# A graph network layer on one core: the short group of edges moved from the end to the start, and one set of nodes instead of two after the last edges

## The chip, the cores and the metric

The kernel runs on one core of a Trainium2 chip. The metric is the device time in microseconds (us), taken as the median of several runs. One further execution is recorded by the hardware profiler; its rows are the "trace" and its summary "the page". The engines are TensorE (PE; PEld is its weight load), VectorE (DVE), ScalarE (ACT), GpSimd (POOL) and SyncE (SP). "Granted clock" is the share of its full clock that TensorE was given.

## The reference

There are 6250 nodes with 256 features, and 206250 edges sorted by their target node (100000 edges in both directions and one loop per node). Everything is float32.

```python
h = relu(layernorm(x))                                # the layer's input
polarity = clip(edge_attr[:, 0:1], 0, 1); raw = edge_attr[:, 1:]          # 64 features of an edge
e = relu(raw @ W_e1.T + b_e1) @ W_e2.T + b_e2
edge_emb = (e * (polarity + 0.01)) @ W_le.T + b_le
msg  = relu(h[src] + edge_emb)
aggr = segment_sum(msg, dst, num_segments=6250)
g = (h + aggr) @ W_g1.T + b_g1
out = x + relu(layernorm(g) * ln_g + ln_b) @ W_g2.T + b_g2
```

## The kernel before

**Tiles.** An edge tile is 128 edges. Four tiles make a block (`S = 4`), six blocks a group (`L = 6`, 3072 edges), and two blocks a pair, which is what one load of `raw` brings (256 KB, L237, on SP's queue). 206250 edges are 67 whole groups and 426 edges over, so there are 403 blocks, `NB = NF * L + 1`: group 67, the last, has one block, number 402, and the last pair (201) is half empty. A unit `u` is two tiles, half a block; there are 806 units.

**Work on an edge.** `first_layer(q)` (L239 to L261) multiplies a pair's raw features with `W_e1`, in four matmuls of 512 columns (L250); ACT writes three of the four results out (L259), DVE one (L256). `edge_part(u)` (L266) multiplies with the product of `W_e2` and `W_le` (L274), and DVE writes the message out with its bias (L279). In the first 22 units every third message is written by ACT without the bias (L277, `plain`), which DVE adds later (L607). `whole(u)` (L601) multiplies by the polarity and adds the gathered source row (DVE, L609, two steps), and ACT takes the relu (L614; for the last unit in two halves, L612). `add_up(b)` (L616) sums a block's edges by target: each of the four tiles is multiplied with a selector of 32 rows (L626), accumulated in PSUM over the group's blocks. The selectors are made by DVE, one step per block (L589), from each edge's row number within its group (`rel`, L488). When a group is complete, `keep(g)` (L633) copies its sums out (L638, or L640 for the last but one).

A matmul of float32 operands appears in the trace as two passes: a unit is 8 passes of L274, a pair's first layer 8 of L250, a tile of the sums 2 of L626.

**Order.** The order is written out by hand (`tc.manual_schedule()`), and each engine keeps it. At first, `LEAD = 22` units run beside the normalisation of the nodes, whose result goes to device memory (`hb_d`). From then on a loop runs over `u`: `forward(u)` (L306) does the unit and, when `u % 4 == TURN` (TURN = 1), a turn for pair `u // 4` (`turn_of`, L291): first layers two pairs ahead, the sums that are due, and loads four pairs ahead. In the middle of the run (`by_two`) every other turn does two pairs at once. After `forward`, the loop makes `whole` for units some distance behind (18 at first, 1 at the end), two per step until it has caught up, and one step of a queue of small jobs (`piece`, `due`). Among these are, right after the lead, `first_rows` (L479), `strips` (L768: `rel`, and the selectors of groups 0 and 1 are queued), and `row_numbers`. The selectors of group g + 2 are queued when group g's first block is summed. PSUM tiles come from a pool of seven (`psz`), and the two accumulators of the sums from another (`pd`).

**Source rows.** Rows `h[src]` are gathered from `hb_d` by POOL, 128 at a time (L560), in step with PE and at most 20 units ahead. The first four units' rows (`RAW`) are gathered from `x` itself and normalised separately (L460 to L466, L605).

**Nodes.** A set of nodes is 128 rows; the 49th has 106. A set is finished when the last group that can hold its edges is kept: `node_work(w)` (L674) makes selectors (L692), adds the groups' sums into the transposed node rows (`rows_of`, L720 to L728), and then runs three steps some units apart: `one` (`first`, L165: the matmul with `W_g1`, L170, bias, statistics, normalisation L180), `two` (`second`, L183: transposes L186, relu L189) and `three` (`third`, L193: matmul L196, the sum with x, L198, and the store, L201).

**The end.** Set 47 ends with group 66 and set 48 with group 67. Both are held back in `ending` and written out after the loop: the sums of set 47 (L726), the first part of those of set 48 (L710), `one` of set 47, the last block's sums, the second part of set 48, then `two`, `one` and `three` of the two in turn. For these two the bias `b_g1` is put into PSUM by a matmul of its own (L168) ahead of L170.

Of the kernel before, what the change touches and what calls it, by code (L numbers as in the profile page):

```python
# [33 lines left out]
NB = NF * L + 1  # L34
# [3 lines left out]
MARGIN = 768  # L38
DEG = E // N
# [16 lines left out]
def group_of(b):  # L56
    return b // L


def blocks_of(g):  # L60
    return range(g * L, min((g + 1) * L, NB))


def windows_of(g):

    lo = (GE * g - MARGIN) // DEG
    hi = (GE * (g + 1) + MARGIN) // DEG
    return [w for w in range(NW) if w * P <= hi and (w + 1) * P > lo]
# [29 lines left out]
def gnn_kernel(ctx: ExitStack, tc: tile.TileContext, x, src_c, dst_c, dst_r, pol_c, raw_t, w_e1t, w_e2,  # L98
# [50 lines left out]
    def finish_nodes(nd, ps, w, n):  # L149
# [15 lines left out]
        def first(aT, bias_by_pe=False):  # L165
            ph = ps()
            if bias_by_pe:
                nc.tensor.matmul(ph[:n, 0, :], ones[0:1, :n], bg1_b[0:1], start=True, stop=False)  # L168
            for c in range(2):
                nc.tensor.matmul(ph[:n, 0, :], aT[:, c, :n], wg1_s[:, c, :], start=c == 0 and not bias_by_pe, stop=c == 1)  # L170
            hs = nd.tile([P, D], F32, name="hs")
            if bias_by_pe:
# [7 lines left out]
            nc.vector.tensor_scalar(hs[:n], hb[:n], mv[:n, 0, 0:1], rs[:n], op0=ALU.subtract, op1=ALU.mult)  # L180
# [32 lines left out]
        return turn, first, second, third, load_x, offset  # L213
# [4 lines left out]
    with fast:  # L218
# [20 lines left out]
        def first_layer(q):  # L239

            bs = [b for b in (2 * q, 2 * q + 1) if b < NB]
# [5 lines left out]
            for c in range(2):  # L247
                for s, b in enumerate(bs):
# [4 lines left out]
            for c in range(2):  # L253
                for s, b in enumerate(bs):
# [7 lines left out]
        def plain(u):  # L262

            return u < LEAD and u % 3 == 1
# [41 lines left out]
        def forward(u):  # L306

            edge_part(u)
            if u % 4 == TURN:
# [19 lines left out]
        nc.scalar.dma_start(out=src_0, in_=src_c[:, :2 * RAW])  # L329
# [9 lines left out]
        nc.gpsimd.iota(mid, pattern=[[GE, NG]], base=GE // 2, channel_multiplier=0, allow_small_or_imprecise_dtypes=True)  # L339
# [4 lines left out]
        for u in range(RAW):  # L344
            hg[u] = hx_p.tile([P, 2, D], F32, name="hg")
            for i in range(2):
                nc.gpsimd.indirect_dma_start(
                    out=hg[u][:, i, :], out_offset=None, in_=x,
                    in_offset=bass.IndirectOffsetOnAxis(ap=src_0[:, 2 * u + i:2 * u + i + 1], axis=0))
        full = NF * L * S  # L350
# [4 lines left out]
        with tc.tile_pool(name="p1", bufs=4) as p1, tc.tile_pool(name="p1x", bufs=11) as p1x:  # L355
            parts = list(chunks())
            xts, mvs = {}, {}
            units = iter(range(LEAD))
# [97 lines left out]
            for n, u in enumerate(units):  # L456
                for m in range(n * RAW // 2, (n + 1) * RAW // 2):
                    row_stats(p1, P, 2, lambda i: hg[m][:, i, :], mv_0[:, 2 * m:2 * m + 2, :])
# [4 lines left out]
            for u in range(RAW):  # L463
                for i in range(2):
                    k = 2 * u + i
                    nc.scalar.activation(hg[u][:, i, :], hg[u][:, i, :], AF.Relu, bias=nm_0[:, k:k + 1],  # L466
# [12 lines left out]
        def first_rows():  # L479

            pb = ps().rearrange("p a b -> p (a b)")[:, :NG * S].rearrange("p (g j) -> p g j", j=S)
            nc.tensor.matmul(pb[:, :NF, :], ones[0:1, :],
                             dst_f[0:1, :full].rearrange("o (g r) -> o g r", r=L * S)[:, :, :S], start=True, stop=True)
            nc.tensor.matmul(pb[:, NF, :], ones[0:1, :], dst_f[0:1, full:], start=True, stop=True)
            nc.scalar.activation(base_b, pb, AF.Copy)

        def rows_of_edges():
            nc.vector.tensor_tensor(  # L488
                rel[:, :full].rearrange("p (g k j) -> p g k j", k=L, j=S),
                dst_f[:, :full].rearrange("p (g k j) -> p g k j", k=L, j=S),  # L490
                base_b[:, :NF, :].rearrange("p g (o j) -> p g o j", o=1).to_broadcast([P, NF, L, S]), ALU.subtract)
            nc.vector.tensor_tensor(rel[:, full:], dst_f[:, full:], base_b[:, NF, :], ALU.subtract)
# [21 lines left out]
        def by_group(i, op):  # L514
            def step():
                nc.vector.tensor_reduce(far[:, i, :NF], dst_f[:, :full].rearrange("p (g r) -> p g r", r=L * S),
                                        axis=AX.X, op=op)
                nc.vector.tensor_reduce(far[:, i, NF:], dst_f[:, full:], axis=AX.X, op=op)
            return step

        def by_row(i, op):
            def step():
                nc.vector.tensor_reduce(ends[:, i:i + 1], rel, axis=AX.X, op=op)
# [477 lines left out]
```

## Time and profile before

| | us |
|---|---|
| median of 3 runs | 2513.2 |
| lowest and highest run | 2512.73, 2515.78 |
| time of the profiled execution | 2537.35 |
| its span, first to last instruction | 2535.6 |
| TensorE busy | 2368.3 (93%) |
| VectorE busy | 1657.0 (65%) |
| POOL busy | 1634.3 (64%) |
| ScalarE busy | 983.4 (39%) |
| mean granted clock | 0.967 |

The page gives busy times over the whole span. The other views answer for a part: the timeline gives instructions in order of time, with the idle time before them and what ended it; the waits give these idle times grouped; the chain follows what ended last back in time; the windows give busy times and the granted clock by stretch. A busy TensorE is not one at its peak, and "issue" in a list of waits is time in which the engine waited for nothing that the profile shows.

### The profile page before, as it was taken

What the parts mean: (1) busy time and instruction counts of PE and PEld (TensorE: products, weight loads), DVE (VectorE), ACT (ScalarE), POOL (GpSimd) and SP (SyncE); (2) the same over time, 40 slices, a digit from 0 to 9 for tenths busy, and PEclk for the clock granted to TensorE, in tenths of its full rate; (3) what the DMA queues carried; (4) which work ended last, traced back from release to release, by engine and by line L of the source; (5) the groups of instructions that cost most, each with busy time, mean ns of one, the idle gap of its engine ahead of it and who ended that gap; (6) DMA issues with size and microseconds to landing.
All of it is one profiled execution on the core that took longest, in us unless ns stands there. A gap on an engine that the chain in (4) does not pass through costs nothing.

```text
span 2535.6 us, 35656 instructions
## 1 busy us (share of the span) xinstructions
PE 2368.3 (93%) x12382; PEld 1669.2 (66%) x12382; DVE 1657.0 (65%) x3975; ACT 983.4 (39%) x1710; POOL 1634.3 (64%) x1675
## 2 busy tenths in 40 slices
PE   9989999999999999999999999999999999999978
PEld 6666666676766666666766766666766666666646
DVE  7866566666767666665666666666766666666736
ACT  7433333333433433343333333333433333333313
POOL 7666666666666666666666666666666666666661
PEclk9999999999999999999999999999999999999979
DMA  9444344433443443434343444344334334433441
GB/s 308 132 119 121 105 126 119 125 119 106 120 134 115 126 119 102 132 112 127 120 129 112 127 117 120 107 123 121 117 115 128 118 113 118 126 115 109 121 117 41
DMA packets 156226, 309.23 MB, mean 122 GB/s; under 512 B 33327, under 2 KB 78088, under 8 KB 156040
## 3 DMA queue, kind: packets, MB, share of 16 engines
q0 software_dynamic: 77376, 211.39, 28.8%
q1 hardware_dynamic: 77364, 92.23, 11.6%
q10 hardware_dynamic: 1300, 3.28, 0.4%
q8 instruction: 98, 1.61, 0.3%
q14 instruction: 88, 0.72, 0.1%
HBM read 293.92 MB, written 12.85 MB: 121 GB/s over the span
## 4 chain that ended last, share of the span: by engine, by line
PE 86%; issue 6%; DVE 5%; another core or an unknown queue 1%; ACT 1%; DVEq 0%; ACTq 0%
PE pz L274 53%; PE pz L250 17%; PE pd L626 10%; PE pz L726 2%; PE pz L170 2%; PE pz L196 2%; DVE hg L609 2%; DVE msg L279 1%; ACT e L259 1%; PE pz L186 1%; DVE st L141 0%; DVE e L256 0%; DVE sel L589 0%; ACT xt L388 0%
## 5 line engine op out<-in xcount | busy, mean ns | idle before, releaser
L560 POOL DMA_INDIRECT hg<-hb_d,src_s x1604 | 1589.3, 991 | 842.5 <-issue 481.3
L274 PE MATMUL pz<-wc_s,e 128*128 128x256 f32 x6448 | 1484.4, 385 | 34.3 <-issue 26.7
L274 PEld LDWEIGHTS pz<-wc_s,e 128*128 128x128 f32 x6448 | 1220.1, 192 | 303.9 <-issue 95.2
L614 ACT ACTIVATE hg<-hg 128x512 f32<-128x512 f32 x805 | 507.1, 631 | 934.3 <-DVE hg L609 760.2
L279 DVE TENSOR_TENSOR msg<-pz,bc_s 128x512 f32<-128x512 f32 x799 | 547.1, 686 | 233.7 <-remote 86.8
L609 DVE SCALAR_TENSOR_TENSOR hg<-msg,pol_s,hg 128x256 f32<-128x256 f32 x1612 | 697.0, 480 | 0.4
L256 DVE TENSOR_SCALAR e<-pz,vecs 128x512 f32<-128x512 f32 x201 | 150.4, 748 | 568.7 <-PE pz L250 192.3
L250 PE MATMUL pz<-raw,we_s 64*128 64x512 f32 x1612 | 480.2, 661 | 24.3 <-issue 18.3
L259 ACT ACTIVATE e<-pz,vecs 128x512 f32<-128x512 f32 x605 | 376.3, 685 | 318.0 <-remote 112.9
L626 PE MATMUL pd<-hg,sel 128*32 128x256 f32 x3216 | 280.5, 389 | 82.8 <-issue 74.6
L250 PEld LDWEIGHTS pz<-raw,we_s 64*128 64x128 f32 x1612 | 170.5, 198 | 240.9 <-issue 176.4
L626 PEld LDWEIGHTS pd<-hg,sel 128*32 128x32 f32 x3216 | 116.0, 110 | 264.2 <-issue 215.0
L589 DVE SCALAR_TENSOR_TENSOR sel<-iota_w,zero_c,rel 128x128 f32<-128x128 f32 x403 | 138.6, 344 | 0.0
L638 ACT ACTIVATE ms<-pd 128x256 f32<-128x256 f32 x66 | 25.3, 384 | 257.9 <-PE pz L274 92.8
L726 PE MATMUL pz<-s,ms 128*128 128x128 f32 x548 | 74.6, 280 | 6.1 <-issue 5.6
L726 PEld LDWEIGHTS pz<-s,ms 128*128 128x128 f32 x548 | 71.1, 194 | 11.6 <-issue 7.7
L701 DVE SCALAR_TENSOR_TENSOR hT<-hT,zero_c,stb 128x128 f32<-128x128 f32 (+1 forms) x196 | 67.1, 343 | 2.3 <-issue 2.3
L170 PE MATMUL pz<-wg_s,hT 128*128 128x256 f32 (+1 forms) x196 | 51.6, 386 | 7.0 <-DVE hT L728 4.7
L196 PE MATMUL pz<-wg_s,nT 128*128 128x256 f32 (+1 forms) x196 | 51.2, 381 | 1.3 <-issue 0.6
L170 PEld LDWEIGHTS pz<-wg_s,hT 128*128 128x128 f32 (+1 forms) x196 | 36.1, 190 | 16.1 <-DVE hT L728 7.5
L196 PEld LDWEIGHTS pz<-wg_s,nT 128*128 128x128 f32 (+1 forms) x196 | 37.0, 190 | 7.7 <-issue 1.7
L392 POOL TENSOR_TENSOR hb<-xt,rows_b 128x256 f32<-128x256 f32 (+1 forms) x49 | 34.2, 729 | 12.0 <-issue 5.4
(98 smaller groups left out, 415.4 us busy)
## 6 DMA issues: line engine op xcount, KB each, us to landing
raw<-in_raw_t_dram SPq DMA_DIRECT2D x202, 256.0 KB
hg<-hb_d,src_s POOLq DMA_INDIRECT x1604
stb<-st_d SPq DMA_DIRECT2D x49, 128.0 KB
hb_d<-hb SPq DMA_DIRECT2D x12, 512.0 KB
xt<-in_x_dram SPq DMA_DIRECT2D x48, 128.0 KB
hT<-in_x_t_dram SPq DMA_DIRECT2D x48, 128.0 KB
out_dram<-ot SPq DMA_DIRECT2D x48, 128.0 KB
xt<-in_x_dram SPq DMA_DIRECT2D x11, 512.0 KB
```

The costliest lines, as they stand in the source:

```text
L196: nc.tensor.matmul(po[:n, 0, :], nT[:, c, :n], wg2_s[:, c, :], start=c == 0, stop=c == 1)
L250: z = nc.tensor.matmul(pe[s, c], we1_s[s * F:(s + 1) * F, c * P:(c + 1) * P], raw[q][s * F:(s + 1) * F, :], start=True, stop=True)
L256: nc.vector.tensor_scalar(e1[b][:, c, :], pe[s, c], be1_s[:, c:c + 1], 0.0, op0=ALU.add, op1=ALU.max)
L259: nc.scalar.activation(e1[b][:, c, :], pe[s, c], AF.Relu, bias=be1_s[:, c:c + 1])
L274: last_z = nc.tensor.matmul(pz[:, i, :], e1[b][:, c, k:k + P], wc_s[:, c, :], start=c == 0, stop=c == 1)
L279: nc.vector.tensor_add(msg[u], pz, bc_s)
L560: g = nc.gpsimd.indirect_dma_start(out=hg[u][:, i, :], out_offset=None, in_=hb_d, in_offset=bass.IndirectOffsetOnAxis(ap=src_s[:, 2 * u + ...
L589: nc.vector.scalar_tensor_tensor(sel[g][:, k * S:(k + 1) * S, :], iota_w.rearrange("p (o w) -> p o w", o=1).to_broadcast([P, S, W]), zero_ ...
L609: nc.vector.scalar_tensor_tensor(hg[u][:, i, :], m[:, i, :], pol_s[:, 2 * u + i:2 * u + i + 1], hg[u][:, i, :], op0=ALU.mult, op1=ALU.add)
L614: nc.scalar.activation(hg[u], hg[u], AF.Relu)
L626: z = nc.tensor.matmul(acc[g][j * W:(j + 1) * W, :], sel[g][:, k * S + j, :], m[:, j % 2, :], start=k == 0, stop=b == blocks_of(g)[-1])
L726: nc.tensor.matmul(pa[:, c, :n], ms[g][:, c * P:(c + 1) * P], box["sel2"][i][:, :n], start=i == 0, stop=i == len(gs) - 1)
```

## The change

The blocks are numbered anew. Block 0 is void: it has no edges and nothing is computed for it. Block 1, alone, is group 0 (the first 512 edges). Groups 1 to 67 have six blocks each, and the last of them holds the padding. Every group from the first on ends with a pair, the last pair (201) is full, and the first pair (0) has one real block. Units run from 2 to 807 (`U0 = 2`), still 806 of them; all that counted units from 0 now counts from `U0`. As pairs are still turned at `u % 4 == 1`, the first layer of pair q + 2 comes two units earlier, counted from the first unit, and the very first unit has a turn of its own. The first loop step after the lead is `u = 24`, so the first turn with two pairs comes at the 24th unit, where no sums are due yet; the first sums, of 20 tiles, come at the 32nd. Before, 8 tiles were summed at the 26th unit and 16 at the 34th.

At the end only set 48 is held back; the margin by which edges may lie before their expected place is cut from 768 to 512 for the last group, so that set 47 needs nothing of it and ends with group 66, which now closes six blocks before the last. Set 48's part from group 66 and its bias are put into PSUM before the last units' messages are whole. The last group's sums are copied half by ACT and half by DVE, and set 48's normalisation is done in two halves. The host lays out the edges accordingly. The core of the diff:

```diff
-NB = NF * L + 1
+NB = NF * L + 2
+SP = S * P
+LAST = 512
+U0 = 2
 def group_of(b):
-    return b // L
+    return (b + L - 2) // L
 def blocks_of(g):
-    return range(g * L, min((g + 1) * L, NB))
+    return range(max(1, 2 + (g - 1) * L), 2 + g * L)
 def windows_of(g):
-    lo = (GE * g - MARGIN) // DEG
-    hi = (GE * (g + 1) + MARGIN) // DEG
+    a, b = (SP + GE * (g - 1), SP + GE * g)
+    lo = (a - (LAST if g == NG - 1 else MARGIN)) // DEG
+    hi = (b + MARGIN) // DEG
...
+        def bias():
             ph = ps()
-            if bias_by_pe:
-                nc.tensor.matmul(ph[:n, 0, :], ones[0:1, :n], bg1_b[0:1], start=True, stop=False)
+            nc.tensor.matmul(ph[:n, 0, :], ones[0:1, :n], bg1_b[0:1], start=True, stop=False)
+            return ph
+        def first(aT, begun=None):
+            ph = ps() if begun is None else begun
...
-            nc.vector.tensor_scalar(hs[:n], hb[:n], mv[:n, 0, 0:1], rs[:n], op0=ALU.subtract, op1=ALU.mult)
+            for h in ([slice(0, P), slice(P, D)] if begun is not None else [slice(0, D)]):
+                nc.vector.tensor_scalar(hs[:n, h], hb[:n, h], mv[:n, 0, 0:1], rs[:n], op0=ALU.subtract, op1=ALU.mult)
...
-            bs = [b for b in (2 * q, 2 * q + 1) if b < NB]
+            bs = [b for b in (2 * q, 2 * q + 1) if 1 <= b < NB]
...
-            if u % 4 == TURN:
+            if u % 4 == TURN or u == U0:
                 turn_of(u // 4)
...
-            units = iter(range(LEAD))
+            units = iter(range(U0, U0 + LEAD))
...
+            nc.vector.tensor_scalar(far[:, 1, NG - 1:], far[:, 1, NG - 1:], float(MARGIN - LAST), None, op0=ALU.add)
...
-                    acc[g] = pd[:, g % 2, :] if g < NG - 1 else ps()[:, 0, :]
+                    acc[g] = pd[:, g % 2, :]
...
-                    if g != NG - 2:
-                        nc.scalar.activation(ms[g], acc.pop(g), AF.Copy)
+                    a = acc.pop(g)
+                    if g < NG - 1:
+                        nc.scalar.activation(ms[g], a, AF.Copy)
                     else:
-                        nc.vector.tensor_copy(ms[g], acc.pop(g))
+                        nc.scalar.activation(ms[g][:, :P], a[:, :P], AF.Copy)
+                        nc.vector.tensor_copy(ms[g][:, P:], a[:, P:])
...
+                def begin():
+                    sums_of(gs[:-1])
+                    box["ph"] = bias()
...
-                if gs[-1] < NG - 2:
-                    return lambda: at(now + 2, rows_of)
-                ending[gs[-1] - NG].append((sums_of, halves_out, rows_of, one, two, three, gs))
+                if gs[-1] < NG - 1:
+                    return lambda: at(now + 2 - (gs[-1] == NG - 2), rows_of)
+                ending.append((begin, sums_of, halves_out, one, two, three, gs))
...
-                lag = max(LEAST, LEAD - RAW - u // SHRINK) + (by_two(u // 4) and (u + 1) % 8 == TURN)
-                ready_for = min(u + 1 - lag, 2 * (u + 1 - LEAD))
+                lag = max(LEAST, LEAD - RAW - (u - U0) // SHRINK) + (by_two(u // 4) and (u + 1) % 8 == TURN)
+                ready_for = min(u + 1 - lag, U0 + 2 * (u + 1 - U0 - LEAD))
...
+            while steps:
+                steps.popleft()[1]()
+            for begin, sums_of, halves_out, one, two, three, gs in ending:
+                begin()
+            while made < NU:
+                whole(made)
+                made += 1
+            add_pairs(last=True)
+            for begin, sums_of, halves_out, one, two, three, gs in ending:
+                sums_of(gs[-1:])
+                halves_out()
+                one()
             while todo:
                 now = min(todo)
                 for fn in todo.pop(now):
                     fn()
-            while steps:
-                steps.popleft()[1]()
-            before, last = ending[-2], ending[-1]
-            for sums_of, halves_out, rows_of, one, two, three, gs in before:
-                rows_of()
-            for sums_of, halves_out, rows_of, one, two, three, gs in last:
-                sums_of(gs[:-1])
-            while made < NU:
-                whole(made)
-                made += 1
-            for sums_of, halves_out, rows_of, one, two, three, gs in before:
-                one()
-            add_pairs(last=True)
-            for sums_of, halves_out, rows_of, one, two, three, gs in last:
-                sums_of(gs[-1:])
-                halves_out()
-            for sums_of, halves_out, rows_of, one, two, three, gs in before:
-                two()
-            for sums_of, halves_out, rows_of, one, two, three, gs in last:
-                one()
-            for sums_of, halves_out, rows_of, one, two, three, gs in before:
-                three()
-            for sums_of, halves_out, rows_of, one, two, three, gs in last:
+            for begin, sums_of, halves_out, one, two, three, gs in ending:
                 two()
                 three()
```

More of the change, by code (lines that the diff above doesn't have):

```diff
@@ L211, in offset @@
             nc.vector.scalar_tensor_tensor(xt[:n, h], xt[:n, h], zero_c[:n], bg2_b[:n, h], op0=ALU.add, op1=ALU.add)
-        return turn, first, second, third, load_x, offset
+        return turn, bias, first, second, third, load_x, offset
     NU = 2 * NB
@@ L522, in step @@
             def step():
-                nc.vector.tensor_reduce(ends[:, i:i + 1], rel, axis=AX.X, op=op)
+                nc.vector.tensor_reduce(ends[:, i:i + 1], rel[:, S:], axis=AX.X, op=op)
             return step
@@ L679, in node_work @@
                 far_apart = (3, 5, 4) if gs[-1] < NG - 3 else (2, 3, 2)
-                turn, first, second, third, load_x, offset = finish_nodes(nd, ps, w, n)
+                turn, bias, first, second, third, load_x, offset = finish_nodes(nd, ps, w, n)
                 def spread():
@@ L928, in nodes @@
             nc.sync.dma_start(out=ac[:n], in_=acc_d[bass.ds(w * P, n), :])
-            turn, one, two, three, load_x, offset = v["finish_nodes"](sk, lambda: sp1.tile([P, 1, D], F32, name="ps_a"), w, n)
+            turn, _, one, two, three, load_x, offset = v["finish_nodes"](sk, lambda: sp1.tile([P, 1, D], F32, name="ps_a"), w, n)
             xt = load_x()
```

91 lines of the change are left out of this document (44 added, 47 removed).

## The prediction

> **What bounds the kernel now.** I read the page's first and fourth parts, then the list of waits of TensorE, then the stretches in which TensorE was not full: the start, the middle of the span and the end.
>
> ```profile
> span 2535.6 us, 35656 instructions
> ...
> PE 2368.3 (93%) x12382; PEld 1669.2 (66%) x12382; DVE 1657.0 (65%) x3975; ACT 983.4 (39%) x1710; POOL 1634.3 (64%) x1675
> ...
> PE 86%; issue 6%; DVE 5%; another core or an unknown queue 1%; ACT 1%; DVEq 0%; ACTq 0%
> ```
>
> TensorE (PE) is the bound, busy 93% of the span and 86% of the chain that ended last; DVE, ACT and POOL stay at 65% or less. The change leaves its work alone (the same 806 units of two edge tiles, the same first layers; two small matmuls of the last node sets and one bias fewer). So the time can move only where PE waits, or where something stands behind PE's last work. The waits:
>
> ```profile
> PE pd L626 <- issue: 74.6, 126, 1.7
> PE pz L274 <- issue: 26.7, 45, 1.7
> PE pz L250 <- issue: 18.3, 29, 1.7
> ```
>
> These 119.6 us are waits for nothing that the profile shows. One stretch is special (columns: stretch, its length, then busy time and count of PE, PEld, DVE, ACT and POOL, the granted clock, DMA share, GB/s):
>
> ```profile
> 2439.62:2470.59 30.97, 16.24 (x36) 9.34 (x36) 1.33 (x4) 2.04 (x4) 19.73 (x21) 0.52 0.32 93
> ```
>
> 36 matmuls at the 0.22 us step of the rows below need 7.9 us; 30.97 passed, 23.1 too many. The profiled execution took 2537.35 us, the median of the runs is 2513.2: 24.15 apart, about this one hole. I therefore take the hole as the profiled execution's own, make the sum as a difference against that execution (2537.35), and apply it to 2513.2.
>
> **Part 1: the start.** The rows of PE (start, duration, line, count of passes, idle time before and its releaser):
>
> ```profile
> 14.14 3.62 PE L274 MATMUL pz<-wc_s,e 128*128 128x256 f32 x16
> 18.69 1.99 PE L250 MATMUL pz<-raw,we_s 64*128 64x512 f32 x8 [0.93 <-DMA raw<-in_raw_t_dram]
> ...
> 64.96 1.99 PE L250 MATMUL pz<-raw,we_s 64*128 64x512 f32 x8
> ...
> 74.94 1.99 PE L250 MATMUL pz<-raw,we_s 64*128 64x512 f32 x8
> 80.74 0.64 PE L626 MATMUL pd<-hg,sel 128*32 128x256 f32 x8 [3.81 <-DVE sel L589]
> ...
> 84.69 2.45 PE L250 MATMUL pz<-raw,we_s 64*128 64x512 f32 x4 [0.50 <-DVE msg L279]
> ```
>
> A unit (8 passes) costs 3.62/2 = 1.8, a pair's first layer 1.9 to 2.0. At 18.69 PE waited 0.93 for the edge rows of pair 2. In the changed order PE has one block's first layer (0.95) and one unit (1.8) less to do before that load lands, because pair 0 holds one real block and pair 2 is asked for after one unit instead of two. The loads ahead of it on SP's queue are the same, so it lands when it did: PE waits 0.93 + 2.75 = 3.7 us. **Loss 2.75.** Nothing wins it back before 64.96, since PE was busy 45.44 of the 46.27 us from there on (columns as above):
>
> ```profile
> 18.69:64.96 46.27, 45.44 (x200) 33.56 (x200) 40.95 (x135) 37.28 (x79) 34.17 (x48) 1.00 0.92 311
> ```
> The later pairs' loads are issued one unit earlier relative to the work and stay covered.
>
> Then comes the one place where VectorE (DVE) bounds: 74.94 to 87.06. PE did 16 passes of L250 twice (2 x 1.92) and 16 of L626 (1.0) in 12.1 us: **7.3 us lost**, first for the row selectors of the first sums, then for PSUM tiles. DVE there (start, duration):
>
> ```profile
> 70.51 0.69 DVE L279 TENSOR_TENSOR msg<-pz,bc_s 128x512 f32<-128x512 f32 x1
> 71.11 0.68 DVE L605 TENSOR_TENSOR hg<-hg,rows_b 128x512 f32<-128x512 f32 x1
> 71.83 0.88 DVE L609 SCALAR_TENSOR_TENSOR hg<-msg,pol_s,hg 128x256 f32<-128x256 f32 x2
> 72.62 0.69 DVE L605 TENSOR_TENSOR hg<-hg,rows_b 128x512 f32<-128x512 f32 x1
> ...
> 80.25 0.35 DVE L589 SCALAR_TENSOR_TENSOR sel<-iota_w,zero_c,rel 128x128 f32<-128x128 f32 x1
> 80.51 0.69 DVE L279 TENSOR_TENSOR msg<-pz,bc_s 128x512 f32<-128x512 f32 x1
> ...
> 87.17 0.75 DVE L256 TENSOR_SCALAR e<-pz,vecs 128x512 f32<-128x512 f32 x1 [1.10 <-PE pz L250]
> ...
> 101.37 0.68 DVE L279 TENSOR_TENSOR msg<-pz,bc_s 128x512 f32<-128x512 f32 x1
> ```
>
> From start to start a message costs 0.60, a pair of L609 0.79, a selector 0.26. The message of the 23rd unit stands at 70.51, that of the 32nd at 101.37: 30.9 us for nine units, with 15 selectors and 13 pairs of L609 between them. In the changed order, counted from the instruction lists, there are 6 selectors (group 0 has one block, so 7 are due instead of 12, and group 2's come later) and 12 pairs: 9 x 0.26 + 0.79 = 3.1 less. The idle 1.10 goes, and a wait of about 0.5 comes, since the first layers of pairs 8 and 9 now follow each other with no sums between and eight tiles go into seven PSUM buffers. So 30.9 - 3.1 - 1.1 + 0.5 = 27.2. When DVE reaches the 23rd unit is between 0 (its own list sets it) and 2.75 later (PE's delay goes through); I take the middle, 1.4. The 32nd message then comes at 70.5 + 1.4 + 27.2 = 99.1, **2.3 earlier** than before. The first sums, now 20 tiles after the 32nd unit, find their selectors made. PE follows DVE there through its buffers, so I take -2.3 for PE. Bounds: +2.75 if PE is the bound and nothing is won back, 2.75 - 7.3 = -4.5 if the whole stall goes. The selectors put off fall where DVE has gaps.
>
> **The clock is the price.** Grid slices (columns as above):
>
> ```profile
> 78.95:82.36 3.41, 1.40 (x18) 0.56 (x20) 3.37 (x7) 0.18 (x1) 3.02 (x2) 0.99 0.26 77
> 82.36:85.77 3.41, 2.91 (x7) 1.12 (x8) 3.41 (x10) 2.60 (x5) 2.58 (x3) 0.50 0.32 84
> 85.77:89.19 3.42, 3.42 (x9) 1.77 (x6) 2.32 (x7) 2.31 (x5) 2.63 (x3) 0.51 0.39 113
> 584.09:587.50 3.41, 1.56 (x7) 1.41 (x8) 1.55 (x4) 2.31 (x4) 1.18 (x2) 1.00 0.19 59
> 587.50:590.92 3.42, 3.42 (x21) 3.12 (x21) 3.42 (x9) 1.89 (x3) 2.50 (x4) 1.00 0.27 77
> ```
>
> A slice in which PE was busy 1.40 of 3.41 is followed by two at half clock; one with 1.56 is not. So about 45% busy is the edge. The new wait of 3.7, or the waits for PSUM of about 2 near 75 and 95, will put some slice under it: one slice at half clock costs 3.41/2 = 1.7. Bounds 0 to three slices, 5.1. I take one. The start comes to -2.3 + 1.7 = **-0.6**.
>
> The Trainium skill, "TensorE: Matmul & The Clock Gate", Part 1, has PE throttled to half after at least one idle window of about 3.4 us. By that rule a wait of 3.7 would seldom hold a whole window, no slice would be lost, and the sum would end 1.7 lower. The slice at 78.95, with 41% busy, speaks against it.
>
> **Part 2: the end.** The chain of waits, and ScalarE's (ACT) rows:
>
> ```profile
> 2515.46 1.99 PE pd L626 x32
> ...
> 2518.01 1.16 PE pz L726 x8
> ...
> 2520.67 1.07 PE pz L170 x4
> ...
> 2523.07 0.69 PE pz L710 x4
> ...
> 2524.69 1.06 PE pz L170 x4
> ...
> 2526.98 0.56 DVE hs L180
> ```
>
> ```profile
> 2519.10 0.63 ACT L614 ACTIVATE hg<-hg 128x512 f32<-128x512 f32 x1 [2.87 <-DVE hg L609]
> 2520.36 0.75 ACT L612 ACTIVATE hg<-hg 128x256 f32<-128x256 f32 x2 [0.62 <-DVE hg L609]
> ...
> 2524.12 0.81 ACT L189 ACTIVATE nT<-pz,vecs 128x128 f32<-128x128 f32 x2 [1.10 <-PE pz L186]
> ```
>
> PE's last unit ends at T = 2515.46; the span ends 20.1 later. Two node sets stand in that tail now, one in the changed kernel.
>
> Moved ahead of T: 24 passes of sums (16 + 4 tiles stood behind T, 8 stay: 24 x 1.99/32 = 1.5), the set of nodes 47 with 8 passes of L726 (1.1) and L170 (1.07). T comes **3.7 later**; DVE and ACT keep up, because the chain of set 47 lies beside the last three units.
>
> Behind T in the new order: message (0.6), L609 of the last two units (0.8 each, the first frees ACT at T + 1.4), ACT's relu (0.63), then ACT's two steps for set 47, which stand ahead in its queue (0.81), the last relu in halves (0.75): T + 3.6. The last sums and the copy of the group, half on ACT and half on DVE (under 0.36), put the second matmul pair of the last set at T + 4.1, against 2523.07 = T + 7.6 before. From there 12.5 us remained. L170 then started 1.62 after it, because the bias stood between; with the bias ahead it starts after its first half is read, about 0.85: 0.8 less. The normalisation L180 (0.56) in halves lets transposes and nT start early: half a step, 0.5, an estimate (bounds 0 and 0.9). T + 4.1 + 12.5 - 1.3 = T + 15.3 against T + 20.1: 4.8 less. With T 3.7 later: **-1.1**, bounds -2.5 (the moved sums partly fill waits) and +0.5 (the halves bring nothing and ACT's queue holds the last relu).
>
> The rest is free: the void block's load lies on SP beside other work, one more scalar step in the check runs on DVE in a stretch with gaps; each index load has four columns more, against 1612.
>
> **Sum.** -0.6 - 1.1 = -1.7: 2535.65 on the scale of the profiled execution, 2511.5 on that of the runs.
>
> **Rivals.**
>
> *The instruction feed decides (slower).* q8 is PE's instruction queue:
>
> ```profile
> q8 instruction: 98, 1.61, 0.3%
> ```
>
> 98 blocks of 16.4 KB, 256 instructions each, and 119.6 us of "issue" waits, 1.2 us per block, most before L626, which uses up instructions fastest. The change shifts where blocks end against the sums by some 56 instructions (two units 32, one block's first layer 8, its sums 16, with weight loads). If six more blocks end in sums, each costs 1.2 and about half of them a clock slice (0.85): +12.3, 2523.8; from four on the result is over 0.2% slower. The same mechanism with six fewer gives 2499, so it is a draw around the forecast. For it: 200 such waits (126 + 45 + 29) stand against 98 blocks. Against: sums and blocks drift past each other several times in the run, which evens out. The Trainium skill, "Runtime: NRT & Kernel Launch", Instruction fetch mechanics, states the refill in blocks of 256 instructions and calls the crossing mostly hidden; by that the change could not move it. The 119.6 us are against hidden, but no row shows the fetch itself.
>
> *The start gains whole (faster).* No slice falls under 45% and the stall near 80 goes entirely: -4.5 at the start, -1.5 at the end, -6.0: 2507. For it: the grid's phase is open, and a wait cut in two by a slice's end may leave both above the edge. Against: 3.7 us is about the 3.81 of the L626 row that half clock followed.
>
> *Nothing comes of it.* PE keeps its total, the late start eats the tail: +2.75 + 1.7 - 1.1 and part of the stall won back: 2513 to 2516.5.
>
> **Chances.** Forecast with its own range (2508.2 to 2514.5) and the third rival, all within 0.2%, 0.43 together; start whole or fewer blocks in sums 0.37; feed on the slow side or two more clock slices 0.20. 0.2% (5 us) is about what a measurement of this kernel can tell from no change. The range reaches to both feed cases without their ends: 2502 to 2519.5.
>
> **What would show it.** After: an L250 near 18.7 with 3 to 4 us of idle before it, released by the raw load; no idle of 3.8 released by sel; the 32nd unit's message near 99; T to the end of the span 15.3; L168 ahead of the last L626. It fails if the issue sum moves by more than 8 us, or the clock in 15 to 30 us falls for two slices or more.

## The result and the profile after

The changed kernel took 2527.33 us (median of 9 runs, 2520.49 to 2533.47), the kernel before 2513.20 in the same series (2504.55 to 2517.68): ratio 1.0042, 95% interval 1.0026 to 1.0059. The medians lie 14.1 us apart; the ratio gives 10.6 us (6.5 to 14.8). Forecast were 2511.5 and a range up to 2519.5. The measurement was then repeated in further series, where the two kernels ran side by side each time:

| series | before, us | changed, us | ratio (95%) | PE waits for "issue" |
|---|---|---|---|---|
| first | 2513.20 | 2527.33 | 1.0042 (1.0026 to 1.0059) | yes |
| e9 | 2549.96 | 2550.85 | 1.0002 (0.9982 to 1.0021) | yes |
| e5 | 2180.94 | 2182.08 | 1.0006 (0.9997 to 1.0015) | none |
| e13 | 2180.43 | 2181.82 | 1.0008 (0.9999 to 1.0017) | one, 1.7 us |
| e16 | 2180.98 | 2182.25 | 1.0006 (0.9997 to 1.0015) | one, 1.7 us |

So there are two things to explain: a small loss of 1.1 to 1.4 us, which comes in all three series without issue waits (each interval by itself still holds no change; the three agree in sign and size), and the 14 us of the first series, which came in no other.

The page of the changed kernel, and its waits of TensorE (total, times, longest):

```profile
span 2525.4 us, 35622 instructions
...
PE 2355.5 (93%) x12376; PEld 1661.5 (66%) x12376; DVE 1654.3 (66%) x3978; ACT 983.3 (39%) x1710; POOL 1637.2 (65%) x1675
...
q8 instruction: 98, 1.61, 0.3%
```

```profile
PE pd L634 <- issue: 69.0, 117, 1.7
PE pz L282 <- issue: 31.8, 49, 2.3
PE pz L258 <- issue: 17.7, 30, 2.2
...
PE pz L258 <- DVE msg L287: 6.5, 8, 2.3
...
PE pz L258 <- DMA raw<-in_raw_t_dram: 2.3, 1, 2.3
```

The first three lines sum to 118.5 us, against 119.6 before, and the instruction queue again moved 98 blocks. The wait for `sel` of 3.8 is gone, and waits of L258 for `msg` have come. The timeline of PE at the start, in the stretch that DVE bounded, and at the end (start, duration, line, passes, idle time before):

```profile
13.82 1.89 PE L282 MATMUL pz<-wc_s,e 128*128 128x256 f32 x8
18.03 1.99 PE L258 MATMUL pz<-raw,we_s 64*128 64x512 f32 x8 [2.32 <-DMA raw<-in_raw_t_dram]
...
70.44 2.85 PE L258 MATMUL pz<-raw,we_s 64*128 64x512 f32 x12
75.59 1.76 PE L258 MATMUL pz<-raw,we_s 64*128 64x512 f32 x4 [2.31 <-DVE msg L287]
...
94.92 1.12 PE L258 MATMUL pz<-raw,we_s 64*128 64x512 f32 x2 [1.31 <-DVE msg L287]
96.58 1.12 PE L258 MATMUL pz<-raw,we_s 64*128 64x512 f32 x2 [0.54 <-issue]
...
2505.34 3.72 PE L282 MATMUL pz<-wc_s,e 128*128 128x256 f32 x16
...
2513.64 0.80 PE L720 MATMUL pz<-s,ms 128*128 128x106 f32 x4 [0.37 <-ACT ms L649]
2514.47 1.11 PE L177 MATMUL pz<-wg_s,hT 128*106 128x256 f32 x4
```

The load of pair 2 is waited for, the two first layers in a row stall twice on PSUM tiles that DVE frees, and PE's last unit ends at T = 2509.06, so the span ends at T + 16.3. DVE's messages of the 23rd and the 32nd unit:

```profile
71.22 0.68 DVE L287 TENSOR_TENSOR msg<-pz,bc_s 128x512 f32<-128x512 f32 x1
...
99.08 0.68 DVE L287 TENSOR_TENSOR msg<-pz,bc_s 128x512 f32<-128x512 f32 x1
```

### The profile page after: what moved, and what is told of

It is laid out like the page before. It is cut to its first block, busy times and chain, and to the rows that moved or that the text cites. A ratio compares the mean times of both kernels' runs of the same rounds, so it can differ in the third digit from the quotient of the medians.

```text
span 2525.4 us, 35622 instructions
## 1 busy us (share of the span) xinstructions
PE 2355.5 (93%) x12376; PEld 1661.5 (66%) x12376; DVE 1654.3 (66%) x3978; ACT 983.3 (39%) x1710; POOL 1637.2 (65%) x1675
## 4 chain that ended last, share of the span: by engine, by line
PE 84%; DVE 6%; issue 5%; another core or an unknown queue 2%; ACT 1%; DMA 1%; POOL 0%; SPq 0%; DVEq 0%; ACTq 0%; POOLq 0%
PE pz L282 52%; PE pz L258 17%; PE pd L634 10%; DVE hg L617 2%; PE pz L740 2%; PE pz L177 2%; PE pz L204 2%; DVE msg L287 2%; ACT e L267 1%; PE pz L194 0%; DMA raw<-in_raw_t_dram 0%; DVE sel L597 0%; DVE e L264 0%; DVE st L145 0%
## 5 line engine op out<-in xcount | busy, mean ns | idle before, releaser
L258 PE MATMUL pz<-raw,we_s 64*128 64x512 f32 x1612 | 476.7, 648 | 31.6 <-issue 17.7
L267 ACT ACTIVATE e<-pz,vecs 128x512 f32<-128x512 f32 x604 | 374.7, 685 | 301.2 <-PE pz L258 99.1
L634 PE MATMUL pd<-hg,sel 128*32 128x256 f32 x3224 | 274.0, 390 | 73.5 <-issue 69.0
L258 PEld LDWEIGHTS pz<-raw,we_s 64*128 64x128 f32 x1612 | 166.8, 195 | 249.9 <-issue 178.6
```

The lines of the kernel that those rows point to most:

```text
L258: z = nc.tensor.matmul(pe[s, c], we1_s[s * F:(s + 1) * F, c * P:(c + 1) * P], raw[q][s * F:(s + 1) * F, :], start=True, stop=True)
L267: nc.scalar.activation(e1[b][:, c, :], pe[s, c], AF.Relu, bias=be1_s[:, c:c + 1])
L634: z = nc.tensor.matmul(acc[g][j * W:(j + 1) * W, :], sel[g][:, k * S + j, :], m[:, j % 2, :], start=k == 0, stop=b == blocks_of(g)[-1])
```

## The experiments

### e1 to e4: does the place of the instructions, or of the tiles, make the 14 us?

e1 puts 16 matmuls of one element (64 instructions with their weight loads) behind the warm-up of the changed kernel, which takes the later stream about back to where it stood in its blocks of 256 (to some 20 instructions, counted in the traces). e2 and e3 put 48 and 32 of them into the kernel before. e4 makes four tiles of the kernel before wider by the four columns that the change adds.

```diff
+        few = ps()
+        for _ in range(16):
+            nc.tensor.matmul(few[:1, 0, 0:1], ones[0:3, 0:1], ones[0:3, 0:1], start=True, stop=True)
```
```diff
-    src_s = const.tile([P, NT], I32, name="src_s")
+    src_s = const.tile([P, NT + S], I32, name="src_s")[:, :NT]
```

> The changed kernel with 16 more one-element matmuls after the warm-up (64 more instructions on TensorE, weight loads and passes counted), so that its instruction blocks of 256 end at the same places of the work as in the kernel before. Theory 1, the instruction feed: the +14 us come from where blocks end against the sums, so this falls back to 2508 to 2517 us. Theory 2, the work itself (another order of work, whatever the feed): it stays at 2522 to 2532, plus up to 2 us for the matmuls.

> The kernel before with 48 more one-element matmuls after the warm-up (192 instructions, which is 64 less in blocks of 256), so that blocks end where they end in the changed kernel. Theory 1, the feed: slower than before by 10 to 17 us, at 2523 to 2532. Theory 2, the work: 2513 plus the matmuls' own 2 to 5 us, 2515 to 2518.

> The kernel before with 32 more one-element matmuls (128 instructions, half a block): how much the place of the block ends is worth at all. Theory 1, the feed: another time than before by more than 5 us, either way. Theory 2, the work: 2513 plus 1 to 4 us.

> The kernel before with the four arrays per edge tile allocated four columns wider in SBUF (1616 instead of 1612, as in the change; the columns are not used), so that everything allocated behind them moves by 16 bytes a partition each. Theory 3, the addresses: it takes the +14 us, 2522 to 2532. Theories 1 and 2: 2513, within 4 us.

The kernel before took 2548.62 us in this series. e1: 2549.02, ratio 1.0005 (0.9982 to 1.0028). e2: 2555.36, 1.0033 (1.0013 to 1.0054), but its start alone is 9.2 us late in the trace (the first layer ahead of the first sums stands at 84.69, in e4 at 75.50), the cost of the added passes and of half clock among them; 2 to 5 was expected. e3: 2552.17, 1.0016 (0.9992 to 1.0040), start 2.8 late (78.29). e4: 2548.13, 1.0005 (0.9985 to 1.0025). Within the errors no shift of the stream costs more than its own passes here, and the wider tiles cost nothing. Nor can e1 be said to win anything, since e9 shows the plain change equal to before at this level of time too, and the plain change did not run in this series.

### e5 to e8: the same kernels where PE never waits for an issue

e5 is the changed kernel again. e6 gives the last group its old margin (`LAST = MARGIN`), so that sets 47 and 48 both follow the last edge part, with everything else as changed. e7 and e8 take the hurried gathers of the last 24 units out of the changed kernel and of the one before.

```diff
-LAST = 512
+LAST = MARGIN
```
```diff
-                if u >= NU - 24:
-                    gathers(4 * summed + HG)
```

> The changed kernel as it is, on the chip that this call gets. Theory 1 (the feed) and theory 2 (the work) both expect the first comparison again, 8 to 20 us slower than the kernel before. Theory 4, that the difference hangs on the chip or on its state and not on the kernel alone, expects another difference than there: within 6 us of the kernel before, or faster.

> The changed kernel with the last group's margin put back from 512 to 768, so that sets 47 and 48 both wait for the last group and stand in the tail; the start is that of the change. If the tail is worth what its rows say (the span after the last unit 16 us instead of 20, less the work moved ahead), this is 1 to 6 us slower than the changed kernel. If the +14 us come from set 47's steps among the last units, it is 10 us or more faster than it.

> The changed kernel without the two lines that issue all gathers still allowed, unpaced, in the last 24 units: there TensorE nearly stands still for some 30 us in every trace. If the unpaced gathers are what it stands still for, the time falls by 10 to 22 us against the changed kernel and the stretch goes from the trace. If the stretch has another cause, within 4 us.

> The same two lines taken out of the kernel before. If the unpaced gathers are the cause, 10 to 22 us faster than before; and if the change made that stretch worse, this and the changed kernel without the lines come out within 5 us of each other. Else within 4 us of before.

e5: 2182.08, 1.0006. e6: 2190.78, 1.0044 (1.0030 to 1.0058), 8.7 above e5. e7: 2182.51, 1.0008 (0.9999 to 1.0017). e8: 2180.28, 0.9996 (0.9987 to 1.0005). The whole level is 330 to 370 us lower than in the other series and there is no issue wait. e6 loses more than the 1 to 6 expected. From PE's last unit (2162.76 + 3.72) to the end of its span (2188.2) pass 21.7 us instead of 16.3, up to 2 of them because the last two matmul rows run at half clock (2.08 and 2.04 for 1.0 to 1.1). Besides, a load of edge rows comes 3.96 late near the end of the run, where two sets' loads stand ahead of it on SP's queue, and its first layer then runs at half clock too (3.41 for 1.99). So e6 does not price the tail set alone. The hurried gathers cost and gain nothing measurable here; e7 and e8 were made for the near stand-still of PE shortly before the end, which this series does not have, so whether the gathers cause it was not tested.

e8 gives the kernel before without issue waits, e13 (below) the changed one. PE in the stretch, first e8, then e13:

```profile
67.79 0.71 PE L482 MATMUL pz<-dst_f,ones 1*128 1x268 f32 x2
68.34 0.28 PE L484 MATMUL pz<-dst_f,ones 1*128 1x4 f32 x2
68.55 5.45 PE L274 MATMUL pz<-wc_s,e 128*128 128x256 f32 x24
73.92 1.99 PE L250 MATMUL pz<-raw,we_s 64*128 64x512 f32 x8
79.72 1.94 PE L626 MATMUL pd<-hg,sel 128*32 128x256 f32 x16 [3.81 <-DVE sel L589]
81.59 4.19 PE L250 MATMUL pz<-raw,we_s 64*128 64x512 f32 x8
...
101.86 1.93 PE L626 MATMUL pd<-hg,sel 128*32 128x256 f32 x32
103.72 1.99 PE L250 MATMUL pz<-raw,we_s 64*128 64x512 f32 x8
```

```profile
19.12 1.99 PE L258 MATMUL pz<-raw,we_s 64*128 64x512 f32 x8 [3.03 <-DMA raw<-in_raw_t_dram]
...
64.58 7.17 PE L282 MATMUL pz<-wc_s,e 128*128 128x256 f32 x32
71.68 2.85 PE L258 MATMUL pz<-raw,we_s 64*128 64x512 f32 x12
76.83 1.76 PE L258 MATMUL pz<-raw,we_s 64*128 64x512 f32 x4 [2.30 <-DVE msg L287]
...
80.45 0.71 PE L489 MATMUL pz<-dst_f,ones 1*128 1x268 f32 x2
81.00 0.28 PE L491 MATMUL pz<-dst_f,ones 1*128 1x4 f32 x2
...
96.15 1.12 PE L258 MATMUL pz<-raw,we_s 64*128 64x512 f32 x2 [1.31 <-DVE msg L287]
97.82 1.12 PE L258 MATMUL pz<-raw,we_s 64*128 64x512 f32 x2 [0.55 <-DVE msg L287]
98.87 2.37 PE L634 MATMUL pd<-hg,sel 128*32 128x256 f32 x40
101.17 1.99 PE L258 MATMUL pz<-raw,we_s 64*128 64x512 f32 x8
```

These two kernels must be compared at equal work, not at equal unit. Counted from the start, e8 has done 208 passes of units and 64 of first layers when its stretch begins at 74.00, e13 192 and 60 at 71.75: 16 x 0.224 + 4 x 0.239 = 4.5 less work. The two short matmuls of the row numbers (L482 and L484, now L489 and L491) count too: they hold PE for 0.9, and e8 has them behind it at that point, e13 still ahead. So e13 has 5.4 less work done, 2.25 earlier: it is 3.2 behind. At the stretch's end e8 has done 272, 96 and 48 passes of sums at 105.71, e13 256, 92 and 40 at 103.16, and both have the short matmuls behind them: 5.0 less work, 2.55 earlier, so 2.5 behind. (A pass of a unit takes 7.17/32 = 0.224, of a first layer 0.239, of the sums 0.06.) **In this pair the stretch gave PE 0.7 back, where 5.05 was forecast** (from a loss of 2.75 to a gain of 2.3).

### e9 to e12: which part of the start costs

e9 is the changed kernel again. e10 asks for pair 2 two loads earlier; in e11 ACT instead of DVE writes four more messages (DVE adds their bias some 18 units later); e12 is that edit in the kernel before.

```diff
             load_rows(1)
+            load_pair(2)
             load_rows(2)
             load_rows(3)
-            load_pair(2)
```
```diff
-            return u < U0 + LEAD and u % 3 == 1
+            return u < U0 + LEAD + 12 and u % 3 == 1
```

> The changed kernel again. Two theories of the +14 us of the first chip. 'Feed': wherever PE waits about 120 us for 'issue', the shifted instruction stream costs some 10 us more, and on a chip without such waits nothing; then this run is +8 to +16 us against the kernel before if issue waits show, and 0 to +3 if not. 'Only start and end': the change costs +1 to +3 us on every chip (late start +3 before the stretch, about -1 at the end), and the rest on the first chip was something else; then +0 to +4 with issue waits too.

> The changed kernel with the edge rows of pair 2 asked for two loads earlier on SP's queue. Theory of the late start: PE's wait for that load (2.3 in the trace of after, 1.5 in another) goes and the time falls 1 to 2 us below e9. Rival (DVE sets the stretch from 65 to 100 us, so that PE's delay ahead of it is given back there anyway): within 0.7 us of e9, with more idle time released by msg in its place.

> The changed kernel in which ACT instead of DVE writes four more messages out (units 25, 28, 31, 34; their bias is added by DVE some 18 units later). Theory: DVE bounds the stretch, the waits of L258 for msg (4.2 us there without issue waits) fall to 1 to 2, and the time falls 2 to 3 us below e9. Rival (the stretch is set by PSUM tiles freed by ACT, or the added steps on DVE come back): within 0.7 us of e9.

> The same edit in the kernel before (units 22, 25, 28, 31). Theory: the wait of 3.8 us for selectors shrinks to under 2 and the two slices at half clock behind it (3.2 us) go, so the time falls 3 to 6 us below the kernel before, more than in e11, because only the kernel before has those slices to lose. Rival (the selectors, not the messages, set it): the wait stays above 3 and the time within 1 us.

e9: 2550.85, 1.0002 (0.9982 to 1.0021). e10: 2551.43, 1.0008 (0.9986 to 1.0030). e11: 2549.93, 1.0002 (0.9982 to 1.0022). e12: 2551.29, 1.0012 (0.9995 to 1.0028). The intervals are 5 us to each side, so the times decide nothing on 2 us; they do decide against a loss of 8 to 16 us in this series, which has issue waits. The traces say more. In e10 the wait for the load is gone and one of 2.8 for `mvx` (DVE) has come. In e11 PE waits 2.86 for a message of ACT in the place of 2.31 for one of DVE. In e12 the wait for `sel` falls from 3.81 only to 3.30. Each edit moved the wait to the engine that now frees the PSUM tile or makes the selector last; by the traces the theory of e10, e11 and e12 falls; the times agree with their rivals but could not have shown 2 us.

### e13 to e15: the stream's place once more, and both edits of the start

e13 is the changed kernel, e14 the kernel of e1, e15 the edits of e10 and e11 together.

> The changed kernel again, beside e14 on one chip. If the place of the instruction blocks decides on some chips, this one is 8 to 16 us above the kernel before where e14 is not. If it does not, both lie within 4 us of each other; on a chip without issue waits both are 0 to 3 us above.

> The changed kernel with 64 small passes ahead, which put its later instructions back to where they stood in their blocks before the change. If the place of the blocks decides: within 3 us of the kernel before, and 8 us or more under e13 where e13 shows the loss. If not: as e13, plus about 1 us for the passes themselves.

> The changed kernel with pair 2 asked for two loads earlier and four more messages written by ACT. Theory of the mis-sized start: on a chip without issue waits 2 to 3 us below e13 and 1 to 2 below the kernel before; on a chip with them the same, hidden in an error of 4 us. Rival (the stretch stays bound by PSUM tiles, now freed by ACT, as a wait of 2.9 for an ACT message in e11 hints): within 1 us of e13.

e13: 2181.82, 1.0008 (0.9999 to 1.0017). e14: 2182.25, 1.0008 (0.9999 to 1.0017). e15: 2182.94, 1.0011 (1.0002 to 1.0020). This series had next to no issue waits, so e13 and e14 say nothing on the 14 us. e15 is not faster than e13: its waits are 2.9 for a message of ACT, 2.1 for `mvx`, and a slice at half clock. No version of the start beat the kernel before.

### e16 to e18: the end alone, and the first turn later

e16 is the changed kernel. e17 is the kernel before with set 48's bias made ahead and its normalisation in halves, both sets still in the tail. e18 is the changed kernel with the first turn one unit later.

```diff
+            for h in ([slice(0, P), slice(P, D)] if begun is not None else [slice(0, D)]):
...
                 sums_of(gs[:-1])
+                begin()
```
```diff
-            if u % 4 == TURN or u == U0:
+            if u % 4 == TURN or u == U0 + 1:
```

> The changed kernel on one more chip. Theory: start +2.6, end -1.0, so +1 to +2 us where no issue waits stand, and the same within an error of 4 to 5 where they do. Rival: the 14 us of the first chip come again, +8 to +16 with issue waits.

> The kernel before with one part of the change alone: set 48's bias is put into PSUM ahead of the last messages and its normalisation is done in two halves; both sets stay in the tail. Theory: from the second part of set 48's sums to the end of the span 13.3 us before, 1.3 to 1.6 less now, and the time falls by 1 to 1.6. Rival (the end is set by set 47's steps, which stand between them on PE, ACT and DVE): under 0.5.

> The changed kernel with the first turn after the second unit instead of the first, so that PE asks for pair 2 as late as the kernel before does, one block's first layer apart. Theory of the start: the wait for that load falls from 2.3 to 3.0 us to 0.5 to 1.2. If PE's delay counts, the time falls by 1 to 2 against e16; if DVE, which has the same list, sets the stretch from 65 to 100, it is won before and given back there: within 0.7 us.

e16: 2182.25, 1.0006 (0.9997 to 1.0015). e17: 2180.25, 0.9998 (0.9989 to 1.0007). e18: 2187.83, 1.0030 (1.0019 to 1.0041), 5.6 above e16, where 0 to 2 below was expected. PE in the tail, first e8, then e17:

```profile
2157.49 1.93 PE L626 MATMUL pd<-hg,sel 128*32 128x256 f32 x32
...
2165.18 0.69 PE L710 MATMUL pz<-s,ms 128*128 128x106 f32 x4 [0.77 <-ACT ms L638]
...
2166.72 1.11 PE L170 MATMUL pz<-wg_s,hT 128*106 128x256 f32 x4
...
2169.77 0.37 PE L186 MATMUL pz<-ident,hs 106*128 106x106 f32 x2 [1.07 <-DVE hs L180]
2170.73 1.96 PE L196 MATMUL pz<-wg_s,nT 128*106 128x256 f32 x4 [0.59 <-ACT nT L189]
```

```profile
2166.18 0.69 PE L716 MATMUL pz<-s,ms 128*128 128x106 f32 x4 [0.77 <-ACT ms L644]
...
2167.02 1.09 PE L175 MATMUL pz<-wg_s,hT 128*106 128x256 f32 x4
...
2169.92 0.54 PE L192 MATMUL pz<-ident,hs 106*128 106x106 f32 x2 [0.94 <-DVE hs L186]
2171.05 1.11 PE L202 MATMUL pz<-wg_s,nT 128*106 128x256 f32 x4 [0.59 <-ACT nT L195]
```

From the second part of the sums to the matmul with `W_g1` there were 1.54 us and are 0.84: the bias ahead is worth 0.7 from that point on. But the second part of the sums itself starts 8.03 after the last unit instead of 7.61, so 0.3 is left of it. From there to the transposes 3.05 and 2.90, and to the last matmul 4.01 and 4.03: the halves are worth nothing, for what they give the transposes the second step of `nT` takes back. The last matmul ran at half clock in e8 (1.96) and not in e17 (1.11). From the second part of the sums to the end pass 13.3 in e8 and 12.0 in e17, as expected of the edit, but most of that is this clock and not the edit. The time of e17 (-0.7) can't be told from none.

The clock's slices of the stretch (columns as in the prediction: length, then busy time of PE, PEld, DVE, ACT, POOL, granted clock). Each trace has its own grid of slices, which the changes of its granted clock show (at 2175.30 in e13, 78.59 in e18, 77.72 in e7). First e13, then e18, then e7:

```profile
72.68:76.10 3.42, 1.85 (x10) 0.66 (x6) 3.35 (x8) 2.63 (x6) 2.79 (x3) 1.00 0.30 95
76.10:79.51 3.41, 2.68 (x9) 1.47 (x10) 2.21 (x5) 3.30 (x6) 2.51 (x3) 1.00 0.33 90
```

```profile
75.18:78.59 3.41, 1.09 (x6) 0.29 (x2) 3.37 (x7) 2.50 (x6) 2.76 (x3) 1.00 0.38 114
78.59:82.01 3.42, 3.42 (x7) 1.64 (x6) 1.28 (x3) 2.93 (x6) 2.55 (x3) 0.50 0.36 95
82.01:85.42 3.41, 3.41 (x8) 2.20 (x8) 3.34 (x8) 0.84 (x2) 2.49 (x4) 0.50 0.30 99
85.42:88.83 3.41, 3.41 (x10) 2.82 (x9) 2.63 (x6) 1.76 (x4) 2.27 (x2) 0.50 0.31 87
```

```profile
74.30:77.72 3.42, 2.09 (x6) 0.96 (x7) 2.23 (x5) 2.71 (x5) 2.51 (x4) 1.00 0.36 105
77.72:81.13 3.41, 3.41 (x9) 2.29 (x8) 3.34 (x7) 2.02 (x4) 2.80 (x3) 0.50 0.35 93
```

All three kernels wait 2.3 us for the same message. In e13 a slice's end cuts the wait, and the clock stays full. In e7 one cuts it too, the slice behind the cut is 61% busy, and yet one slice at half clock follows. In e18 the wait begins 1.2 us later and falls into one slice, 32% busy: three slices at half clock follow. At equal work they cost 4.9 us, but PE then waits 2.6 less at the second pair of first layers, so the stretch costs 9.3 where e16's costs 7.0. e18 was already 1.4 behind e16 when the stretch began. Together that is 3.7; the traced executions lie 3.5 apart (2184.80 against 2181.31). The 5.6 between the medians is more than the trace explains.

## Why the prediction was wrong, step by step

**The start's wait: right in kind, too dear.** Forecast were a wait of 3.7 and a loss of 2.75. The wait was 2.32 in the trace of the changed kernel, 3.03 in e13, 1.47 in e7 and 0.20 in e6. In e5, e9 and e16 PE ran passes at half rate between 5 and 14 us instead (8 passes of L408 took 3.8 for 2.0), and the load was there when it came. Counting lost time as above, seven traces with the changed start stand at 13.1 to 14.4 us before the stretch (mean 13.7), five with the old one, without the two short matmuls, at 11.2 to 12.8 (mean 12.0): 1.7 us lost, not 2.75.

**The stretch: the step that failed.** "The 32nd message then comes at 99.1" was right in the first trace (99.08; 27.9 us for nine units, 27.2 forecast). "PE follows DVE there through its buffers, so I take -2.3 for PE" was wrong. When DVE writes the 32nd message, at 100.07 in e8 and at 100.32 in e13, PE has done 34 units there and only 32 here: the PSUM tiles that held two units ahead now hold first layers. A unit's message does not tell where PE is when its lead changes. Counted at equal work, the stretch costs 7.0 us in each of the six traces with the changed order that no issue wait disturbs there (e5, e6, e7, e13, e14, e16); 0.9 of it are the two short matmuls, which leaves 6.1. In e4, e8 and e17, which have the old order, it costs 6.2 to 6.9 without them. The wait for PSUM tiles, priced at 0.5, is 2.3 at the first pair of first layers, and 1.3 and 0.5 at the second in most traces. Instead of -5.05 from the 23rd unit on, the stretch brought about -0.4. That DVE bounds it was right: in e7 and e14 a slice at half clock costs PE 1.6 in the middle of it, and the same 7.0 stand at its end.

**The clock: neither the edge nor the price held.** One slice was charged. None fell at these waits in the traces of the unaltered changed kernel (the first, e5, e9, e13 and e16); in e7 and e14, which have the same order there, one did. The kernel before loses one or two there. That gain is within the 6.1 against 6.2 to 6.9. The edge of 45% does not sort the slices. The slice that holds most of the wait was 1.55 busy in e16, 1.77 in the first trace and 1.85 in e13, and full clock followed; it was 2.09 in e7 and 1.96 in e14, and half clock followed. The price of 1.7 per slice is what PE loses at the spot, 1.6 in e7 and e14 and 4.9 for three in e18; part of it or all came back behind, where DVE bounds. What decides whether the clock falls stays open. The Trainium skill, "TensorE: Matmul & The Clock Gate", Part 1, asks for an idle window of about 3.4 us before the clock is halved; by that rule a wait of 2.3 costs none, and the rows of e18 and e7 speak against it as the prediction's did.

**The end: right in the sum.** T comes 6.3 later in e13 than in e8 (2163.84 against 2157.56), of which the start and the stretch are 2.5 in these two, so 3.8 is work moved (3.3 when e17 is taken for e8); 3.7 was forecast. T to the end is 16.3 to 16.5 in every trace of the changed kernel, not 15.3: the second part of the sums starts at T + 4.6 instead of 4.1, and the halves, 0.5 in the sum, are worth nothing (e17). Before it was 20.2 in the first trace and 21.0 in e8. So the end gave between 0 and 0.9, where 1.1 was forecast. The one set less shortens the tail by about 4, but nearly all of it is work that now stands ahead of T.

**The hole: wrong.** It was taken as the profiled execution's own. The changed kernel's trace has it too, at the same place, and so have all ten traces with many issue waits: PE loses 22 to 33 us there within eight units, some 15 to 20 units before the last. e13, without these waits, has none (20 us stretches of the changed kernel, then of e13):

```profile
2420.00:2440.00 20.00, 12.91 (x61) 7.73 (x54) 4.41 (x12) 3.62 (x6) 15.29 (x16) 0.67 0.36 106
2440.00:2460.00 20.00, 11.69 (x29) 3.88 (x28) 5.73 (x14) 2.55 (x6) 7.59 (x8) 0.50 0.20 59
```

```profile
2100.00:2120.00 20.00, 20.00 (x126) 13.92 (x125) 15.27 (x36) 9.25 (x17) 15.43 (x16) 1.00 0.37 101
2120.00:2140.00 20.00, 20.00 (x120) 14.52 (x119) 15.65 (x39) 7.40 (x13) 15.43 (x16) 1.00 0.44 125
```

It comes and goes with the issue waits, whichever of the two kernels runs. The record gives e9, which has both, and e16, which has neither, the same chip number 5, so it is a condition that changes and, as far as that number tells, not the chip alone. The sum did not hang on it, but the 24 us between the profiled execution and the runs should have widened the range.

**The sum.** Start +1.7, stretch -0.4 and end 0 to -0.9 give +0.4 to +1.3; measured were 1.1 to 1.4 where no issue waits stand, inside 0.2%. Forecast was -1.7, with -2.3 from the start and the stretch before the clock, where +1.3 came. The third rival (nothing comes of it) described that case best.

**The 14 us of the first series stay open.** The rival of the instruction feed gave 2523.8, near to what was measured, but its sign in the profile did not come: the issue sum moved by 1.1 us between the two traces, not by more than 8. e9 shows no such loss with issue waits present (at most 5.4 us by its interval), and e2 and e3 no price of a shifted stream beyond the added passes. The traces also speak against its mechanism. The instruction queue moves one block for every 256 instructions of PE in the trace. In each of the ten traces with many issue waits these keep to a place in the turn of eight units (247 instructions), whose fullest quarter holds 51 to 76% of their time; the fullest quarter of a block holds 31 to 42%. Where blocks end is thus not what places them. No trace of the kernel before exists at its 2513: its profiled execution stood 24 above its runs, that of the changed kernel on its runs, so the two traces can't be subtracted for it. Whether the place of the blocks mattered in that first series alone was not settled. So for the miss of the first series the cause is not known: the sum took the issue waits as unchanged by the change, and no run shows that the change lengthened them.

## What to carry to other kernels

Compare two orders of work at equal work done, small matmuls counted too, and not at the same unit's message: an engine's early finish is no gain when the bounding engine has less lead by then. Removing a wait from a stretch that another engine bounds only moves it, and moving a wait by a microsecond against the clock's grid can cost as much again as the wait (2.3 in e18's stretch). Measure a change of 0.1% in more than one series before its sign is believed.

## What the runs showed of the hardware

The same kernel took 2180 us in three series and 2513 to 2550 in others. In the long ones PE waits 109 to 125 us for "issue" in the three largest lines of each trace, about 0.6 us at a time (69.0/117), with half-clock slices behind and a near stand-still shortly before the end; in the short ones there is at most one such wait and PE is busy 99%. The Trainium skill, "Runtime: NRT & Kernel Launch", Instruction fetch mechanics, calls the crossing from block to block mostly hidden: the short series agree, and in the long ones the waits do not recur with the blocks, so nothing here shows the crossing. And a start thinned by one block ran passes at half rate between 5 and 14 us in three of its seven traces, in none of five of the old start. In e16 the granted clock is 0.50 there, from 7.9 to 14.7; in e5 and e9 the trace holds no record of the clock before 14.2 and 14.0 (the windows then print 1.00). What decides it was not tried.
